# A Macaron block on one core: the last three tiles of every expert part put behind a branch

## The chip, the cores and the metric

One core of a Trainium2 chip runs the whole block. The metric is the device time in microseconds of one execution. The kernel before was run three times: 655.76, 656.89 and 658.45 us, median 656.89. A separate execution under the profiler gives the page and the trace.

## The reference

16 sequences of 256 tokens with 128 features, so 4096 tokens. Three steps, each added to the tokens:

```python
x = x + 0.5 * ffn(layernorm(x))
x = x + attention(layernorm(x))      # 16 heads of 8, causal
x = x + 0.5 * ffn(layernorm(x))

def ffn(flat):                       # 8 experts, 256 hidden, best 2 of 8 for each token
    probs = softmax(flat @ gate_w.T)
    weights, idx = top_k(probs, 2)
    weights = weights / sum(weights)
    combine = sum(one_hot(idx, 8) * weights[..., None], axis=1)
    h1, h3 = einsum('nd,ehd->neh', flat, w1), einsum('nd,ehd->neh', flat, w3)
    y = einsum('neh,edh->ned', silu(h1) * h3, w2)
    return einsum('ned,ne->nd', y, combine)
```

The reference runs all eight experts on every token. The kernel runs only the two that each token chose, so it sorts the tokens by expert on the chip. Everything is computed in 32-bit floats, apart from masks and counts.

## The kernel before, in words

The tokens stay in SBUF as eight blocks of 512. Each of the two feed-forward steps is cut into three parts, each with its own routing: blocks 0, 1 to 3 and 4 to 7 before the attention (`ahead`), blocks 0 to 3, 4 to 6 and 7 after it (`after`). A part has a scratch tensor in DRAM for the sorted inputs (`part.x`, in the trace `rows_x`) and one for the experts' outputs (`part.y`, `rows_y`).

*Routing* (`route_in_steps`, lines 330 to 441) finds each token's two experts, counts them per expert, and gives each of the two choices a row in `part.x`. An expert's rows start at a new tile of 128 rows, so its last tile is filled up with rows that no token owns. How many tiles this takes depends on the data; with `ht` tiles of tokens it can't exceed `2 * ht + 7`, and that is the number of tiles that the kernel always runs (`part.nj`, line 59): 15, 31 and 39 tiles for parts of 1, 3 and 4 blocks, 170 over both steps. `upto` holds the running sum of tiles over the experts. From it lines 421 to 434 make `eji`, the expert of each tile; tiles past the last counted one are given to expert 7, run on zeros or left-over rows, and nobody reads their outputs.

*Scatter* (line 449): POOL writes the normalised tokens to their rows, 128 rows for each indirect transfer, two transfers for each tile of tokens. *Experts* (lines 466 to 592): tiles go through in groups of three. SP loads a group (`xg`), PE transposes it (`px`), ACT copies it (`xgT`); for each tile DVE copies the chosen expert's first weights (`wt`, line 502; the expert's number comes from `eji` through a register load, line 483), PE multiplies (`ph`, line 514), ACT and DVE make `silu(h1) * h3` (`gt`, lines 525 and 536), PE multiplies with the second weights (`py`, line 544), ACT copies a group's result and sends it to `part.y` (lines 554 and 555). *Combine* (lines 595 to 623): POOL gathers each token tile's two output rows (`yt`, line 611), and DVE adds them, weighted, to the tokens (line 602), four gathers behind.

`experts_of` (line 655) interleaves a part's tiles with other work. Each turn emits one tile, then one step of `aside` (routing of another part, a piece of the attention's opening), then `rate(j)` transfers from `beside` (the scatter of a later part's rows, or the gathers of an earlier part). A transfer is preceded by a one-element memset called `tick`, which is emitted even when no transfer is left. At turn `part.nj` the next part is prepared by `then()`: its first loads, its first transposes, its first two weight copies. Before this, with `ahead`, all transfers are emitted. After the last turn the remaining transfers are emitted in any case (line 710). Inside these stages the order on PE, POOL, DVE and ACT is the order of emission; SP's order is left to the scheduler.

The last stages, lines 1252 to 1274: the tiles of `after[0]` run beside the scatters for the two later parts, the tiles of `after[1]` beside the gathers of `after[0]`, the tiles of `after[2]` beside the gathers of `after[1]`; then the gathers of `after[2]` follow. Finished blocks are stored by SP (line 1196).

Of the kernel before, what the change touches and what calls it, by code (L numbers as in the profile page):

```python
# [11 lines left out]
FP = mybir.dt.float32  # L12
BF = mybir.dt.bfloat16
I32 = mybir.dt.int32
AF = mybir.ActivationFunctionType
ALU = mybir.AluOpType
# [3 lines left out]
P = 128  # L20
NB, SEQ, D = 16, 256, 128
NH, DK = 16, 8
NE, NHID = 8, 256
NHC = NHID // P
# [11 lines left out]
HT = NT // 2  # L36
JG = 3
NJG = 13


class InTurn:


    def __init__(self, *pools):
        self.pools = itertools.cycle(pools)
# [5 lines left out]
class Part:  # L51


    def __init__(self, first, blocks, scratch):
        self.first, self.blocks = first, blocks
        self.ht = blocks * TPB


        self.nj = 2 * self.ht + NE - 1
        self.ng = -(-self.nj // JG)  # L60
        self.x, self.y = scratch


# [4 lines left out]
def macaron_kernel(  # L68
# [15 lines left out]
    nc = tc.nc  # L84
# [4 lines left out]
    work = ctx.enter_context(tc.tile_pool(name="work", bufs=2))  # L89
# [20 lines left out]
    def load_x(*blocks):  # L110
        for t in blocks:
            nc.sync.dma_start(
                out=xs[t], in_=x[ts(t, BLK), :].rearrange("(c p) d -> p c d", p=P)
            )


    def scratch(name, blocks):
        rows = Part(0, blocks, (None, None)).nj * P
        return tuple(tc.dram_tile([rows, D], FP, name=f"{name}_{s}") for s in "xy")

    places = [scratch(f"rows{i}", n) for i, n in enumerate((1, 3, 4))]
    ZW = 16
    zeros = const.tile([P, ZW * D], FP)
    nc.vector.memset(zeros, 0.0)

    def clear(i, queue=nc.sync):
        rows = places[i][0].rearrange("(p c) d -> p (c d)", p=P)
        n = rows.shape[1]
        for at in range(0, n, ZW * D):
            w = min(ZW * D, n - at)  # L130
            queue.dma_start(out=rows[:, at : at + w], in_=zeros[:, 0:w])
# [8 lines left out]
    w13_f = w13_sb.rearrange("d e w h -> d (e w h)")  # L140
    w2_f = w2_sb.rearrange("p c e d -> p (c e d)")
# [2 lines left out]
    nc.sync.dma_start(out=w2_sb, in_=w2)  # L144
    clear(1)
    load_x(4, 5, 6, 7)
    wq_in = const.tile([D, NG, 4, 32], FP)
    wk_in = const.tile([D, NG, 4, 32], FP)
    wv_sb = const.tile([D, D], FP)
# [7 lines left out]
    ident = const.tile([P, P], FP)  # L157
# [5 lines left out]
    for e in range(NE):  # L163
# [7 lines left out]
        out=before_f,  # L171
        in_=before_f,
# [13 lines left out]
    for blocks in (1, 3, 4):  # L186
        n = blocks * TPB
# [142 lines left out]
    def route_in_steps(part, ps, fine=False, placed_at=None):  # L330
# [33 lines left out]
        rest = new("rest")  # L364
# [7 lines left out]
        d = new("d", [P, ht])  # L372
# [19 lines left out]
        upto = new("upto", [P, NE])  # L392
# [15 lines left out]
        rows = new("rows", [P, 2, ht])  # L408
# [8 lines left out]
        if placed_at is not None:  # L417
            placed_at(rowi)
        yield

        grid = [1, part.ng * 4, NE]
        past = work.tile([1, NJG * 4, NE], FP, tag="g_past", name="past")[:, 0 : part.ng * 4, :]
        nc.vector.tensor_tensor(
            past,
            jgrid[:, 0 : part.ng * 4, :],
            upto[0:1, :].unsqueeze(1).to_broadcast(grid),
            ALU.is_ge,
        )
        if fine:
            yield  # L430
        ej = work.tile([1, NJG * 4], FP, tag="g_ej", name="ej")[:, 0 : part.ng * 4]
        nc.vector.tensor_reduce(ej, past, AX.X, ALU.add)
        eji = work.tile([1, NJG * 4], I32, tag="g_eji", name="eji", bufs=3)
        nc.vector.tensor_scalar(eji[:, 0 : part.ng * 4], ej, float(NE - 1), None, ALU.min)

        den = new("den", [P, ht])
        nc.vector.tensor_scalar(den, ex, 2.0, 2.0, ALU.mult, ALU.add)
        c = new("c", [P, 2, ht], bufs=3)
# [27 lines left out]
    def experts(part, eji):  # L466
# [6 lines left out]
        def load(g):  # L473
            xg = work.tile([P, JG, D], FP, tag="xg", name="xg", bufs=3)
            n = tiles(g)
            nc.sync.dma_start(
                out=xg[:, 0:n, :],
                in_=part.x[g * JG * P : (g * JG + n) * P, :].rearrange("(c p) d -> p c d", p=P),
            )
            loaded[g] = xg  # L480
# [57 lines left out]
        def project(j):  # L538
# [12 lines left out]
            if c == tiles(g) - 1:  # L551
# [7 lines left out]
                    in_=yg[:, 0:n, :],  # L559
                )  # L560

        def fetch():
            load(0)
            load(1)
# [8 lines left out]
        def run():  # L573
            for j in range(part.nj + 2):
                made.at = j
                ph = hidden(j) if j < part.nj else None
                if j < part.nj and j % JG == 0:
                    g = j // JG
                    if g + 2 < part.ng:
                        load(g + 2)  # L580
                    if g + 1 < part.ng:
                        turn(g + 1)
                if j + 2 < part.nj:
                    weigh(j + 2)
                if ph is not None:
                    gated(j, ph)
                if 0 <= j - 2:
                    project(j - 2)
                yield

        made = SimpleNamespace(part=part, fetch=fetch, begin=begin, tiles=run(), begun=False, by_tanh=False)
        return made


# [60 lines left out]
    def experts_of(  # L655
        work,
        beside,
        aside=iter(()),
        side=(0, 0),
        pulls=lambda j: 1,  # L660
        rate=lambda j: 1,
        then=None,
        opened=None,
        ahead=True,
    ):

        following = None

        def transfer():
            nc.gpsimd.memset(tick, 0.0)  # L674
            return next(beside, done)

        done = object()
        with opened or ExitStack() as stack:
            one = 1 if side[1] else 2
            if opened is None:  # L680
                banks = expert_banks(stack, one, 3 if side[1] else 4)
            else:
                banks = work.banks
                more = psum(stack, "ps_h2", 2)
                banks.h = InTurn(banks.h, more)
            if side[0]:
                pools["first"], pools["banks"] = psum(stack, "ps_f", 1), side[0]
            if side[1]:
                pools["side"] = psum(stack, "ps_m", side[1])
            stack.enter_context(manual())  # L690
            if not work.begun:
                work.fetch()
                work.begin(banks)
            work.banks = banks
            for _ in work.tiles:
                j = work.at
                for _ in range(pulls(j)):
                    next(aside, None)
                for _ in range(rate(j) if j >= 2 else 0):
                    transfer()  # L700
                if j == work.part.nj:
                    for _ in aside:
                        pass
                    while ahead and transfer() is not done:
                        pass
                    if then is not None:
                        following = then()
                        following.fetch()
                        following.begin(banks)
            while transfer() is not done:  # L710
                pass
        return following

# [322 lines left out]
    after = [Part(0, 4, places[2]), Part(4, 3, places[1]), Part(7, 1, places[0])]  # L1036
# [155 lines left out]
    def back(part, route, after_block):  # L1192
        return combine(part, route[0], route[2], after_block)

    def store(t):
# [4 lines left out]
    none = lambda t: None  # L1200
    opening, steps, left_routes, left_moves = attention(after)
    tiles = experts(ahead[0], routes[0][1])
    tiles = experts_of(
        tiles,
        second,
        others(),
        (0, 2),
        rate=lambda j: 2,
        then=lambda: experts(ahead[1], routes[1][1]),
    )  # L1210
    tiles = experts_of(
        tiles,
        scatter(ahead[2], xns, routes[2][0]),
        constants(),
        rate=lambda j: 2,
        then=lambda: experts(ahead[2], routes[2][1]),
    )
# [2 lines left out]
        itertools.chain(back(ahead[0], routes[0], none), back(ahead[1], routes[1], none)),  # L1220
        opening(),
        (2, 1),
        pulls=lambda j: int(j >= 14),
    )

    left, right = ExitStack(), ExitStack()
# [20 lines left out]
    with manual():  # L1247
# [4 lines left out]
    tiles = experts_of(  # L1252
        behind[0],
        following(left_moves),
        ending,
        (0, 2),
        rate=lambda j: 2,
        then=lambda: experts(after[1], left_routes[1][1]),
        opened=opened,
    )  # L1260
    tiles = experts_of(
        tiles,
        back(after[0], left_routes[0], store),
        then=lambda: experts(after[2], left_routes[2][1]),
        ahead=False,
    )
    experts_of(
        tiles,
        back(after[1], left_routes[1], store),
        rate=lambda j: 1 + (j % 3 == 0),  # L1270
        ahead=False,
    )
# [42 lines left out]
```

## Time and profile before

| | |
|---|---|
| median of three runs | 656.89 us |
| the profiled execution's own time | 657.1 us |
| its span, first to last instruction | 655.1 us |
| mean granted PE clock | 0.965 |
| PE busy / PE weight loads | 576.9 us (88%) / 484.4 us (74%) |
| DVE / ACT / POOL busy | 448.2 (68%) / 352.7 (54%) / 419.7 (64%) |
| scatter transfers, issue on POOL (L449) | 128, 988 ns each |
| gather transfers, issue on POOL (L611) | 128, 975 ns each |
| group loads `xg` / output writes `rows_y` | 58 each, of them 56 of 192 KB: 2.9 / 2.1 us to landing |

The expert parts lie at about 47 to 79, 79 to 125 and 125 to 202 us, then the attention until about 494 with the first tiles of the next part already among its last batch, then 478 to 560, 560 to 606 and 606 to 629 us, and a tail to 655. Busy shares over the whole span mix these stages, which don't have the same limit; they are best read stage by stage. PE, DVE, ACT, POOL and SP are the five engines; a name with a q is the engine's sequencer or DMA queue. In a timeline row the number in brackets is the idle time of the engine before the row, with what ended it by the profile.

### The profile page before, as it was taken

The page shows a single profiled execution, that of the slowest core. Times are in us where ns is not written, and L with a number is a line of the kernel's source. Part 1 is how long each engine was busy: PE and PEld are TensorE (multiplying, and loading weights), DVE is VectorE, ACT ScalarE, POOL GpSimd, SP SyncE. Part 2 cuts the span into 40 slices and gives each one's busy share as a digit, 9 for nine tenths or more (in the row PEclk, how much of TensorE's full clock was granted, in tenths as well). Part 3 has the DMA queues.
Part 4 walks back from the last instruction along what each step waited for, and adds up shares of the span by engine and source line. Part 5 has one row for each costly group of instructions (what it writes and reads, how often), then busy time and mean ns, then how long its engine had stood idle before and what let it go on. Part 6 is the DMA issues. An engine that isn't in the chain of part 4 may idle for free.

```text
span 655.1 us, 17006 instructions
## 1 busy us (share of the span) xinstructions
PE 576.9 (88%) x6158; PEld 484.4 (74%) x6158; DVE 448.2 (68%) x1405; ACT 352.7 (54%) x730; POOL 419.7 (64%) x862
## 2 busy tenths in 40 slices
PE   4369799999998999999999999999998799999930
PEld 3258699999986677777777766777677799999930
DVE  7754765566665788888887899677646556576742
ACT  6245444446623667777686866675646345444410
POOL 3568889767532666666663437788710884787785
PEclk9989999999996999999999999999999979999985
DMA  8726444454310000000000000000112333456442
GB/s 301 276 86 225 131 125 130 134 137 107 78 42 20 19 14 20 18 18 15 18 18 3 2 2 23 29 30 36 58 38 60 110 110 94 131 148 165 122 121 72
DMA packets 65905, 53.73 MB, mean 82 GB/s; under 512 B 6560, under 2 KB 60576, under 8 KB 65312
## 3 DMA queue, kind: packets, MB, share of 16 engines
q1 hardware_dynamic: 34368, 22.16, 10.8%
q0 software_dynamic: 8192, 16.79, 8.6%
q10 hardware_dynamic: 23264, 13.71, 7.1%
q8 instruction: 50, 0.82, 0.5%
q14 instruction: 31, 0.25, 0.1%
HBM read 25.43 MB, written 27.20 MB: 80 GB/s over the span
## 4 chain that ended last, share of the span: by engine, by line
PE 70%; POOL 8%; DVE 8%; issue 5%; ACT 5%; DMA 2%; DVEq 1%; ACTq 0%; POOLq 0%; SPq 0%
PE ph L514 18%; PE sm L782 12%; PE py L544 8%; PE o L887 7%; PE sw L797 6%; PE sm L809 6%; POOL rows_x L449 4%; PE pl L315 3%; POOL yt L611 3%; PE px L493 2%; PE pt L302 2%; DVE top L813 2%; ACT pT L823 1%; PE pm L868 1%; PE po L925 1%
## 5 line engine op out<-in xcount | busy, mean ns | idle before, releaser
L514 PE MATMUL ph<-xgT,wt 128*128 128x128 f32 x1360 | 184.9, 280 | 8.6 <-DVE wt L502 6.7
L514 PEld LDWEIGHTS ph<-xgT,wt 128*128 128x128 f32 x1360 | 169.3, 196 | 11.7 <-DVE wt L502 5.5
L825 POOL TENSOR_SCALAR_AFFINE_SELECT pT<-pT 128x256 f32<-128x256 f32 x256 | 100.0, 414 | 107.4 <-ACT pT L823 106.3
L813 DVE TENSOR_REDUCE top<-sm 128x3 f32<-128x384 f32 x256 | 130.3, 551 | 54.5 <-PE sm L809 51.4
L449 POOL DMA_INDIRECT rows_x<-xn,rowi x128 | 126.5, 988 | 47.7 <-issue 22.6
L823 ACT ACTIVATE pT<-sw 128x768 f32<-128x768 f32 x128 | 104.0, 812 | 86.2 <-PE sw L797 79.3
L611 POOL DMA_INDIRECT yt<-rows_y,rowi x128 | 124.9, 975 | 28.4 <-issue 15.9
L782 PE MATMUL sm<-kp,qp 32*128 32x256 f32 (+1 forms) x1024 | 127.9, 354 | 3.2 <-ACT kp L758 1.6
L525 ACT ACTIVATE gt<-ph 128x256 f32<-128x256 f32 x165 | 63.2, 384 | 117.4 <-PE ph L514 108.1
L797 PE MATMUL sw<-qm,kp 32*128 32x128 f32 (+1 forms) x1024 | 120.9, 354 | 1.1 <-ACT pT L823 1.1
L782 PEld LDWEIGHTS sm<-kp,qp 32*128 32x128 f32 x1024 | 95.1, 187 | 31.3 <-DVE top L813 10.6
L536 DVE TENSOR_TENSOR gt<-gt,ph 128x256 f32<-128x256 f32 x165 | 68.6, 416 | 59.9 <-ACT gt L525 59.2
L544 PE MATMUL py<-w_sb,gt 128*128 x680 | 104.6, 278 | 3.3 <-ACT yg L554 1.9
L502 DVE COPY wt<-w_sb 128x512 f32 x170 | 75.7, 448 | 36.1 <-issue 25.0
L544 PEld LDWEIGHTS py<-w_sb,gt 128*128 128x128 f32 x680 | 90.5, 194 | 4.1 <-ACT yg L554 2.3
L797 PEld LDWEIGHTS sw<-qm,kp 32*128 32x128 f32 x1024 | 68.6, 189 | 2.8 <-ACT pT L823 1.8
L602 DVE SCALAR_TENSOR_TENSOR x<-yt,c,x 128x128 f32<-128x128 f32 x128 | 45.7, 361 | 18.3 <-DMA yt<-rows_y,rowi 18.0
L887 PE MATMUL o<-pT,vaug 128*32 128x256 f32 (+1 forms) x1024 | 56.2, 335 | 0.0
L809 PE MATMUL sm<-mask_two,ident_b 128*128 128x256 bf16 x256 | 50.8, 281 | 0.0
L250 POOL TENSOR_TENSOR rstd<-ve,neg_half 128x4 f32<-128x4 f32 x24 | 25.3, 1054 | 39.6 <-DVE ve L248 38.7
L887 PEld LDWEIGHTS o<-pT,vaug 128*32 128x32 f32 x1024 | 27.7, 110 | 23.2 <-issue 9.6
L674 POOL MEMSET tick<- 128x1 f32 x269 | 37.3, 139 | 5.7
(124 smaller groups left out, 660.3 us busy)
## 6 DMA issues: line engine op xcount, KB each, us to landing
xg<-rows_x SPq DMA_DIRECT2D x56, 192.0 KB, 2.9
rows_y<-yg ACTq DMA_DIRECT2D x56, 192.0 KB, 2.1
w_sb<-in_w SPq DMA_DIRECT2D x3, 1024.0 KB
x<-in_x SPq DMA_DIRECT2D x8, 256.0 KB, 13.8
rows_x<-xn,rowi POOLq DMA_INDIRECT x128
rows_x<-zeros ACTq DMA_DIRECT2D x2, 1024.0 KB
yt<-rows_y,rowi POOLq DMA_INDIRECT x128
out_y<-x SPq DMA_DIRECT2D x8, 256.0 KB, 3.5
```

The lines of the kernel that those rows point to most:

```text
L449: i = nc.gpsimd.indirect_dma_start(out=part.x, out_offset=bass.IndirectOffsetOnAxis(ap=rowi[:, n, t : t + 1], axis=0), in_=xns[part.first ...
L502: nc.vector.tensor_copy(wt.rearrange("d k h -> d (k h)"), w13_f[:, bass.ds(es[g][c] * (2 * NHID), 2 * NHID)],)
L514: nc.tensor.matmul(out=ph[:, k // NHC, k % NHC, :], lhsT=wt[:, k, :], rhs=xTs[g][:, c, :], start=True, stop=True,)
L544: nc.tensor.matmul(out=ys[g][:, c, :], lhsT=gt[:, hc, :], rhs=w2_f[:, bass.ds(es[g][c] * D + hc * (NE * D), D)], start=(hc == 0), stop=(hc ...
L611: nc.gpsimd.indirect_dma_start(out=yt, out_offset=None, in_=part.y, in_offset=bass.IndirectOffsetOnAxis(ap=rowi[:, n, t : t + 1], axis=0),)
L782: nc.tensor.matmul(out=s[u][:, to], lhsT=qp[r, j, ts(q, P)], rhs=kp[r, SET[j], k], start=(q == 1), stop=False,)
L797: nc.tensor.matmul(out=s[:, u, to], lhsT=kp[r, SET[j], ts(k, P)], rhs=qm[r, j, q], start=True, stop=True,)
L809: nc.tensor.matmul(out=s[u][:, 128:384], lhsT=ident_b, rhs=mask_qk, start=False, stop=True)
L813: nc.vector.tensor_reduce(tops[b % 2][:, j, i0 + u, :], s[u][:, 0:384].rearrange("p (n k) -> p n k", k=P), AX.X, ALU.max,)
L823: nc.scalar.activation(pT, s[:, :, 0:384], AF.Exp, scale=DK**-0.5)
L825: nc.gpsimd.affine_select(out=pT[:, u, 0:256].rearrange("p (n q) -> p n q", q=P), in_=pT[:, u, 0:256].rearrange("p (n q) -> p n q", q=P), ...
L887: nc.tensor.matmul(out=o[32 * i : 32 * i + 32, j // 2, q], lhsT=va[:, kt, 4 * j + i, :], rhs=pTs[i // 2][:, i % 2, at], start=(j % 2 == 0 ...
```

## The change

A part now runs only `2 * ht + 4` tiles always (`part.nj`: 12, 28, 36). The three tiles that can come on top (`SPARE`) are a new function `rest`, whose body stands behind a branch: entered if the routing counted more than `part.nj` tiles. The count is one more element at the end of `eji`. The scratch tensors keep their size, and the last three tiles of each `part.y` are filled with zeros at the start. `experts_of` calls `rest` after a part's turns, before what transfers are left; all five engines load the count and branch. In the stage of `after[1]`'s tiles, the gathers of `after[0]` that are left over after the last turn are no longer emitted at its end (`all_of_them=False`) but come first beside the tiles of `after[2]`. The attention's opening is pulled from turn 11 instead of 14.

```diff
+SPARE = 3
...
-        self.nj = 2 * self.ht + NE - 1
+        self.most = 2 * self.ht + NE - 1
+
+        self.nj = self.most - SPARE
         self.ng = -(-self.nj // JG)
+        self.grid = -(-self.most // JG)
...
+    for _, y in places:
+        nc.sync.dma_start(
+            out=y[y.shape[0] - SPARE * P :, :].rearrange("(p c) d -> p (c d)", p=P),
+            in_=zeros[:, 0 : SPARE * D],
+        )
...
-        eji = work.tile([1, NJG * 4], I32, tag="g_eji", name="eji", bufs=3)
-        nc.vector.tensor_scalar(eji[:, 0 : part.ng * 4], ej, float(NE - 1), None, ALU.min)
+
+        eji = work.tile([1, NJG * 4 + 1], I32, tag="g_eji", name="eji", bufs=3)
+        nc.vector.tensor_scalar(eji[:, 0:n], ej, float(NE - 1), None, ALU.min)
+        nc.vector.tensor_copy(eji[:, NJG * 4 : NJG * 4 + 1], upto[0:1, NE - 1 : NE])
...
+        def rest():
+            counted = nc.values_load(
+                eji[0:1, NJG * 4 : NJG * 4 + 1],
+                min_val=0,
+                max_val=part.most,
...
+            )
+            banks = made.banks
+            few = range(part.nj, part.most)
+            rows = slice(part.nj * P, part.most * P)
+            with tc.If(counted > part.nj):
+                xg = work.tile([P, JG, D], FP, tag="xg", name="xg", bufs=3)
+                nc.sync.dma_start(
+                    out=xg, in_=part.x[rows, :].rearrange("(c p) d -> p c d", p=P)
+                )
+                px = banks.x.tile([P, JG, P], FP, tag="x", name="px")
+                for c in range(SPARE):
+                    nc.tensor.transpose(px[:, c, :], xg[:, c, :], ident)
+                xT = work.tile([D, JG, P], FP, tag="xgT", name="xgT", bufs=2)
+                nc.scalar.copy(xT, px)
+                wt = work.tile([D, SPARE, 2 * NHC, P], FP, tag="w_rest", name="w_rest", bufs=1)
+                py = banks.y.tile([P, JG, D], FP, tag="y", name="py")
+                for c, j in enumerate(few):
...
+                yg = work.tile([P, JG, D], FP, tag="yg", name="yg", bufs=3)
+                nc.scalar.copy(yg, py)
+                nc.scalar.dma_start(
+                    out=part.y[rows, :].rearrange("(c p) d -> p c d", p=P), in_=yg
                 )
...
+        all_of_them=True,
     ):
...
-            while transfer() is not done:
+            work.rest()
+            while all_of_them and transfer() is not done:
                 pass
...
-        pulls=lambda j: int(j >= 14),
+        pulls=lambda j: int(j >= 11),
...
+    gathers = back(after[0], left_routes[0], store)
     tiles = experts_of(
         tiles,
-        back(after[0], left_routes[0], store),
+        gathers,
         then=lambda: experts(after[2], left_routes[2][1]),
         ahead=False,
+        all_of_them=False,
     )
     experts_of(
         tiles,
-        back(after[1], left_routes[1], store),
+        itertools.chain(gathers, back(after[1], left_routes[1], store)),
         rate=lambda j: 1 + (j % 3 == 0),
         ahead=False,
     )
```

The tiles within the branch, left out above at the inner "...", do for each of the three what `turn`, `weigh`, `hidden`, `gated` and `project` do for a tile.

More of the change, by code (lines that the diff above doesn't have):

```diff
@@ L117, in scratch @@
     def scratch(name, blocks):
-        rows = Part(0, blocks, (None, None)).nj * P
+        rows = Part(0, blocks, (None, None)).most * P
         return tuple(tc.dram_tile([rows, D], FP, name=f"{name}_{s}") for s in "xy")
@@ L419, in route_in_steps @@
         yield
-        grid = [1, part.ng * 4, NE]
-        past = work.tile([1, NJG * 4, NE], FP, tag="g_past", name="past")[:, 0 : part.ng * 4, :]
+        n = part.grid * 4
+        grid = [1, n, NE]
+        past = work.tile([1, NJG * 4, NE], FP, tag="g_past", name="past")[:, 0:n, :]
         nc.vector.tensor_tensor(
             past,
-            jgrid[:, 0 : part.ng * 4, :],
+            jgrid[:, 0:n, :],
             upto[0:1, :].unsqueeze(1).to_broadcast(grid),
@@ L430, in route_in_steps @@
             yield
-        ej = work.tile([1, NJG * 4], FP, tag="g_ej", name="ej")[:, 0 : part.ng * 4]
+        ej = work.tile([1, NJG * 4], FP, tag="g_ej", name="ej")[:, 0:n]
         nc.vector.tensor_reduce(ej, past, AX.X, ALU.add)
-        eji = work.tile([1, NJG * 4], I32, tag="g_eji", name="eji", bufs=3)
-        nc.vector.tensor_scalar(eji[:, 0 : part.ng * 4], ej, float(NE - 1), None, ALU.min)
+        eji = work.tile([1, NJG * 4 + 1], I32, tag="g_eji", name="eji", bufs=3)
+        nc.vector.tensor_scalar(eji[:, 0:n], ej, float(NE - 1), None, ALU.min)
+        nc.vector.tensor_copy(eji[:, NJG * 4 : NJG * 4 + 1], upto[0:1, NE - 1 : NE])
         den = new("den", [P, ht])
@@ L560, in project @@
                 )
+        def rest():
[3 more added lines that the diff above has]
+                max_val=part.most,
+                skip_runtime_bounds_check_because="tiles are counted by the routing",
+            )
[15 more added lines that the diff above has]
+                for c, j in enumerate(few):
+                    at = 4 * (j // JG) + j % JG
+                    _, (e,) = nc.values_load_multi_w_load_instructions(
+                        eji[0:1, at : at + 1],
+                        engines=[mybir.EngineType.PE, mybir.EngineType.DVE],
+                        min_val=0,
+                        max_val=NE - 1,
+                        skip_runtime_bounds_check_because="the values are held within the experts",
+                    )
+                    nc.vector.tensor_copy(
+                        wt[:, c].rearrange("d k h -> d (k h)"),
+                        w13_f[:, bass.ds(e * (2 * NHID), 2 * NHID)],
+                    )
+                    ph = banks.h.tile([P, 2, NHC, P], FP, tag="h", name="ph")
+                    for k in range(2 * NHC):
+                        nc.tensor.matmul(
+                            out=ph[:, k // NHC, k % NHC, :],
+                            lhsT=wt[:, c, k, :],
+                            rhs=xT[:, c, :],
+                            start=True,
+                            stop=True,
+                        )
+                    gt = work.tile([P, NHC, P], FP, tag="gt", name="gt", bufs=4)
+                    nc.scalar.activation(gt, ph[:, 0], AF.Silu)
+                    nc.vector.tensor_tensor(gt, gt, ph[:, 1], ALU.mult)
+                    for hc in range(NHC):
+                        nc.tensor.matmul(
+                            out=py[:, c, :],
+                            lhsT=gt[:, hc, :],
+                            rhs=w2_f[:, bass.ds(e * D + hc * (NE * D), D)],
+                            start=(hc == 0),
+                            stop=(hc == NHC - 1),
+                        )
+                yg = work.tile([P, JG, D], FP, tag="yg", name="yg", bufs=3)
+                nc.scalar.copy(yg, py)
+                nc.scalar.dma_start(
+                    out=part.y[rows, :].rearrange("(c p) d -> p c d", p=P), in_=yg
+                )
@@ L589, in run @@
                 yield
-        made = SimpleNamespace(part=part, fetch=fetch, begin=begin, tiles=run(), begun=False, by_tanh=False)
+        made = SimpleNamespace(
+            part=part, fetch=fetch, begin=begin, tiles=run(), rest=rest, begun=False, by_tanh=False
+        )
         return made
```

## The prediction

> **What bounds the kernel now.** I read the chain of waits first, then the busy table by slices, cut again into this kernel's own stages, then the timelines of POOL and PE at the joints. I name the six expert parts A (15 tiles), B (31), C (39) before the attention and D (39), E (31), F (15) after it.
>
> ```profile
> PE 70%; POOL 8%; DVE 8%; issue 5%; ACT 5%; DMA 2%; DVEq 1%; ACTq 0%; POOLq 0%; SPq 0%
> ```
>
> PE carries 70% of the chain, so dropping 18 of 170 tiles looks large. A steady tile repeats every 1.45 us (in B, three tiles from 83.54 to 87.89: 4.35 us), so a part gives up 4.35 us where PE is last, six parts 26 us. The stages say where it is last (columns: stretch, length, busy us of PE, PE loads, DVE, ACT, POOL, granted clock, DMA share, GB/s; B, C, E, F, the end):
>
> ```profile
> 79.00:125.00 46.00, 45.28 (x402) 45.01 (x403) 26.64 (x90) 20.87 (x53) 40.03 (x107) 1.00 0.44 133
> 125.00:188.00 63.00, 61.87 (x529) 59.51 (x527) 42.95 (x130) 34.76 (x89) 40.97 (x87) 1.00 0.40 105
> 560.00:606.00 46.00, 44.92 (x404) 44.76 (x403) 31.40 (x88) 21.31 (x53) 37.08 (x75) 1.00 0.56 150
> 606.00:629.00 23.00, 22.08 (x192) 21.54 (x192) 16.16 (x48) 9.91 (x24) 17.90 (x34) 1.00 0.49 131
> 629.00:655.00 26.00, 0.00 (x0) 0.00 (x0) 6.68 (x19) 0.00 (x0) 16.67 (x26) 0.58 0.30 83
> ```
>
> In the last 26 us PE does nothing: POOL's gathers end the kernel. In B both PE and POOL are nearly full. POOL's timeline settles both places:
>
> ```profile
> 119.58 5.72 POOL L674 MEMSET tick<- 128x1 f32 x33
> ...
> 558.88 3.39 POOL L674 MEMSET tick<- 128x1 f32 x17
> 563.87 1.06 POOL L611 DMA_INDIRECT yt<-rows_y,rowi  x1 [1.59 <-DMA xg<-rows_x]
> ...
> 600.36 1.03 POOL L611 DMA_INDIRECT yt<-rows_y,rowi  x1 [2.09 <-DVE x L602]
> ...
> 609.42 1.04 POOL L611 DMA_INDIRECT yt<-rows_y,rowi  x1 [2.50 <-DVE wt L502]
> ...
> 648.57 0.95 POOL L611 DMA_INDIRECT yt<-rows_y,rowi  x1 [0.30 <-issue]
> ```
>
> B's companion, the scatter of C's rows, ends at 119.58; C's first rows are fetched at 121.45 and transposed at 124.30. From 563.87 there are 64 gathers, one each 1.255 us when nothing holds them: 63 steps, 79.1 us. They take 84.7 to the start of the last, so under 6 us of that stretch is waiting: 2.09 for a buffer that DVE frees late, 2.50 before gather 33, the first to need E's outputs.
>
> **Is the branch entered?** Routing the reference's inputs gives 12, 27, 35, 36, 27, 12 tiles with rows; the new caps are 12, 28, 36, 36, 28, 12. None exceeds its cap, so all six bodies are jumped over and 18 tiles are really gone.
>
> **What the tiles give, by part.** A: B's first rows wait for the scatter that POOL issues back to back from 49.99 to 72.97; it doesn't move. 0. B: C's rows wait for the scatter that starts at 76.06 and ends at 119.58. It follows A's ticks, six fewer x 0.154 = 0.9 us, against a crossing of about 1 us. 0; PE gets 4.35 us of slack. C: PE is busy 61.87 of 63, so 4.35 us come off; the attention opening is pulled three tiles earlier, so nothing of it is pushed past the end. D: it decides when the gathers start, and there POOL is last: the final scatter ends at 558.88 because its places come from the routing near tile 32 of D, which is kept. What goes is six of 17 ticks (3.39/17 = 0.20 each), 1.2 us, and the wait for D's outputs, which come 4.35 us earlier. E: its outputs come about 8 us earlier, so the two waits above go. F: outputs are ready some 15 us before gather 57 needs them. 0.
>
> **What a crossing adds.** Each engine loads the counted tiles into a register, compares, jumps to the other side, waits there for its own earlier work, jumps on. The load has a row, by the experts' numbers that PE and DVE load today (min/median/max ns):
>
> ```profile
> L483 DVEq TENSOR_LOAD <-eji x58: 623/804/2561, 20.8 to 618.9; - x58
> L483 PEldq TENSOR_LOAD <-eji x58: 308/790/2657, 21.0 to 617.6; - x58
> ```
>
> I take 0.8 us. The jumps have no row. [...]
>
> In the built order, the first matmul after the join waits on ACT, DVE and PE together, so I let PE wait for the last engine across. Where it is exposed:
> - C's start: ACT issues B's last output transfer at 125.63 + 0.34, then 1.0: 127.0, against PE's start at 125.42. **+1.6**.
> - C to attention: ACT's last transfer ends at 202.67, crossing 203.7; score matmuls at half clock follow (to about 205), and only then the table load of 1.28 us, which today runs beside them; the first exponential goes from 204.05 to about 206.3. **+2.2**.
> - A's: slack of B. PE will idle from about 72, where A's last tiles run today, until B's rows at 77.5. A gap of 4.27 us ahead of 524.70 shows what follows (columns as above):
>
> ```profile
> 522.00:524.00 2.00, 0.00 (x0) 0.00 (x0) 0.16 (x1) 0.60 (x2) 1.82 (x4) 0.95 0.08 33
> 524.00:526.00 2.00, 1.30 (x6) 1.30 (x7) 1.83 (x5) 1.28 (x4) 1.95 (x5) 0.50 0.15 53
> 526.00:528.00 2.00, 2.00 (x11) 2.00 (x11) 0.42 (x1) 0.89 (x3) 1.81 (x4) 0.50 0.52 154
> ```
>
> Half clock for some 7 us, 3.3 us lost. With the delayed start and a reload of ACT's table (1.28, moved from A) B loses about 4.5 of its 4.35 + 0.6: C still starts near 124.3.
> - POOL, the engine that ends the kernel, crosses three times on its path: full 1.0 at D (ticks wait for each other, so nothing covers the load), about 0.4 at E and at F, where a gather of 0.95 covers the rest.
>
> The three added writes of zeros (0.59 MB on SP's queue, ahead of the attention weights) take 1.5 us of a busy stretch at 380 GB/s; the weights are not used before 90 us, SP's next issue is at 31.84. 0. Moving leftover gathers doesn't shorten POOL's list: the built order has 32 gathers, E's crossing, 12, F's, 20. It merely lets F's weights and first tile pass ahead. 0. Six DVE copies of one element, near 0.2 us each: 0, under ACT's and PE's work.
>
> **Sum, against the profiled execution** (span 655.1, with 2.0 around it 657.1; median of the runs 656.9). C: -4.35 + 1.6 + 2.2 = -0.55. End: 558.88 + 2.2 ticks + 1.0 + 0.76 (the idle that a gather with many waits shows at 126.06) = 562.9; 32 gathers x 1.255 to 603.1; + 0.4 + 0.8 for gather 33, 604.3 (E's outputs land near 603); 39.15 more as today, + 0.4: the last starts at 643.9, not 648.57: -4.7. Together -5.2: **652**. Its own range is 648.5 to 655.5 (C and the end each off by 2).
>
> **Rivals.** [...] (2) *B ends early and PE's clock drops ahead of C.* If B keeps its slack, PE idles 4 us before 124.3 and C starts at half clock: +3.3, 655.3. For it: the rows above; against: the loss at A eats that slack. (3) *Crossings hide.* If PE needn't wait for ACT, C saves 4.35 - 0.4 - 1.0, and POOL's loads run under gathers and ticks: the end -5.8; 648.3. (4) *A body is entered*: where a part stands at its cap, no expert lies less than 5 rows from one more tile; then near +10.
>
> **Chances.** Forecast 0.48, (1) 0.24, (2) 0.13, (3) 0.13, (4) 0.02. This kernel can tell about 0.5% (3.3 us) from no change. Some 0.34 of the forecast's own lies below 653.6, with (3) 0.47 faster; 0.14 of it and most of (2), 0.26 the same; (1), (4) and a rest, 0.27 slower. The range 646.5 to 662 leaves out the upper part of (1) and little else.
>
> **What would show it.** Right: C's first tile still near 124; the first gather near 563, gather 33 near 604, no idle of 2 us within the gathers; PE idle and half clock about 77; POOL's hole at D 1 to 2 us. Wrong: holes of 3 us or more at crossings, C starting late, half clock at its start.

## The result, and the profile after

| | before | after |
|---|---|---|
| median of 20 runs | 657.35 us (653.50 to 662.53) | 655.23 us (650.23 to 663.13) |
| ratio | | 0.9955, 95% interval 0.9933 to 0.9977 |
| profiled execution / span | 657.1 / 655.1 us | 654.5 / 652.8 us |
| mean granted PE clock | 0.965 | 0.942 |
| PE busy | 576.9 us | 561.8 us |

By the ratio the change is worth about -3.0 us, -4.4 to -1.5 (the medians differ by 2.1). Medians are of all executions; ratios leave out the few that ran in a slower state. A second measurement of the same pair gave 0.9941 (0.9910 to 0.9973), -3.9 us. The forecast was -5.2 us and 652.0: the right side, inside the range, and at the edge of what can be told from no change. PE is busy 15 us less, and the kernel gains a fifth of it.

No body was entered: there are 1216 first-weight matmuls, 8 for each of 152 tiles. The stages again, of the kernel after (columns as before: stretch, length, busy us of PE, PE loads, DVE, ACT, POOL, granted clock, DMA share, GB/s; B, C, E, F, the end):

```profile
79.00:121.00 42.00, 41.76 (x357) 41.57 (x357) 22.62 (x82) 19.48 (x47) 36.40 (x97) 0.96 0.41 126
123.50:184.00 60.50, 59.27 (x489) 56.81 (x490) 38.74 (x119) 32.28 (x82) 37.59 (x69) 0.97 0.37 100
556.00:599.00 43.00, 42.53 (x364) 42.08 (x364) 27.22 (x77) 18.67 (x46) 34.61 (x71) 0.96 0.52 143
603.00:620.00 17.00, 16.86 (x140) 16.51 (x140) 12.05 (x34) 7.01 (x18) 14.27 (x26) 0.95 0.42 110
622.00:652.80 30.80, 0.00 (x0) 0.00 (x0) 8.22 (x24) 0.00 (x0) 20.82 (x34) 0.55 0.31 87
```

Each stage is shorter and none of these stretches has the full clock any more (0.95 to 0.97; before, 1.00 in all four); the joints between them are left out. PE's last matmul ends at 620.5 instead of 628.4 us, the span only 2.3 us sooner: POOL's gathers still close the kernel. POOL's timeline of the kernel after, at the places shown of before:

```profile
117.22 3.88 POOL L751 MEMSET tick<- 128x1 f32 x25
...
559.31 1.37 POOL L751 MEMSET tick<- 128x1 f32 x9
...
562.28 0.98 POOL L687 DMA_INDIRECT yt<-rows_y,rowi  x1 [0.91 <-DMA xg<-rows_x]
...
600.20 0.94 POOL L687 DMA_INDIRECT yt<-rows_y,rowi  x1 [3.18 <-DVEq L585]
...
607.21 0.94 POOL L687 DMA_INDIRECT yt<-rows_y,rowi  x1 [0.86 <-DVE x L678]
...
646.49 0.94 POOL L687 DMA_INDIRECT yt<-rows_y,rowi  x1 [0.30 <-issue]
```

The first gather is at 562.28; before it was at 563.87, and the forecast was 562.9. The wait ahead of gather 33 has shrunk from 2.50 to 0.86. The one ahead of gather 28 (600.20) was to go; it has grown from 2.09 to 3.18.

The crossings themselves, in the kernel after (count, then min/median/max in ns, first and last start):

```profile
L576 POOLq TENSOR_LOAD <-eji x6: 293/296/497, 72.4 to 620.6; - x6
L576 DVEq TENSOR_LOAD <-eji x6: 313/314/514, 74.1 to 620.7; - x6
L576 PEldq TENSOR_LOAD <-eji x6: 305/308/309, 75.7 to 619.9; - x6
L576 ACTq TENSOR_LOAD <-eji x6: 278/283/533, 78.2 to 621.5; - x6
```

```profile
L585 POOLq COMPARE_BRANCH  x6: 45/45/45, 73.0 to 621.0; - x6
L585 DVEq COMPARE_BRANCH  x6: 56/56/72, 74.4 to 621.1; - x6
L585 PEldq COMPARE_BRANCH  x6: 215/234/344, 76.1 to 620.3; - x6
L585 ACTq COMPARE_BRANCH  x6: 45/45/45, 78.8 to 621.9; - x6
```

By the medians a load of one value takes 0.28 to 0.31 us, and not the 0.8 of the row for three values; a compare and branch 0.05 to 0.06 us, on PE 0.23. No long hold at one shows: the longest of them lasts 0.34 us, and of the two queues that the page calls instruction, q8 moves 50 packets in both kernels, q14 33 against 31. So nothing is seen of (1), the slower kernel to which the prediction gave 0.24. An engine's own crossing is cheap: load and branch together are 0.33 to 0.37 us on POOL, ACT and DVE, 0.54 on PE. What follows is about what waits for it.

### The profile page after: what moved, and what is told of

Same layout as the page of the kernel before. It is cut to its first block, busy times and chain, and to the rows that moved or that the text cites. A ratio compares the mean times of both kernels' runs of the same rounds, so it can differ in the third digit from the quotient of the medians.

```text
span 652.8 us, 16461 instructions
## 1 busy us (share of the span) xinstructions
PE 561.8 (86%) x5924; PEld 466.2 (71%) x5924; DVE 434.4 (67%) x1375; ACT 340.4 (52%) x700; POOL 413.8 (63%) x840
## 5 line engine op out<-in xcount | busy, mean ns | idle before, releaser
L526 PE MATMUL ph<-xgT,wt 128*128 128x128 f32 x1216 | 171.6, 287 | 12.7 <-ACTq L585 6.6
L526 PEld LDWEIGHTS ph<-xgT,wt 128*128 128x128 f32 x1216 | 157.7, 202 | 16.1 <-ACTq L585 7.4
L537 ACT ACTIVATE gt<-ph 128x256 f32<-128x256 f32 x147 | 56.4, 383 | 112.1 <-PE ph L526 104.0
L548 DVE TENSOR_TENSOR gt<-gt,ph 128x256 f32<-128x256 f32 x147 | 61.2, 416 | 63.8 <-ACT gt L537 63.2
L556 PE MATMUL py<-w_sb,gt 128*128 x608 | 94.0, 279 | 2.1 <-ACT yg L566 1.9
L514 DVE COPY wt<-w_sb 128x512 f32 x152 | 66.8, 442 | 35.0 <-issue 23.8
L556 PEld LDWEIGHTS py<-w_sb,gt 128*128 128x128 f32 x608 | 81.4, 196 | 2.7 <-ACT yg L566 2.3
L505 PE MATMUL px<-ident,xg 128*128 128x128 f32 x152 | 28.6, 301 | 12.7 <-SPq L585 6.6
```

The costliest lines, as they stand in the source:

```text
L514: nc.vector.tensor_copy(wt.rearrange("d k h -> d (k h)"), w13_f[:, bass.ds(es[g][c] * (2 * NHID), 2 * NHID)],)
L526: nc.tensor.matmul(out=ph[:, k // NHC, k % NHC, :], lhsT=wt[:, k, :], rhs=xTs[g][:, c, :], start=True, stop=True,)
L548: nc.vector.tensor_tensor(gt, gt, ph[:, 1], ALU.mult)
L556: nc.tensor.matmul(out=ys[g][:, c, :], lhsT=gt[:, hc, :], rhs=w2_f[:, bass.ds(es[g][c] * D + hc * (NE * D), D)], start=(hc == 0), stop=(hc ...
```

## The experiments

Theory at the start: the crossings take the gain, through PE's wait for the other engines at each join. Rival: the clock takes it, crossing or not. Each ratio is to the kernel before, measured beside it.

**The crossings left out, and the crossings alone.** The first kernel doesn't call `rest`, so a part's optional tiles can't run at all. The second keeps all 170 tiles and places the same body, never entered, behind the same branch; it also keeps the change's small parts, the writes of zeros and the later place of leftover gathers, which the first kernel has too.

```diff
-            work.rest()
```

```diff
-        self.nj = self.most - SPARE
+        self.nj = self.most
...
-            few = range(part.nj, part.most)
-            rows = slice(part.nj * P, part.most * P)
+            few = range(part.nj - SPARE, part.nj)
+            rows = slice((part.nj - SPARE) * P, part.nj * P)
...
-        pulls=lambda j: int(j >= 11),
+        pulls=lambda j: int(j >= 14),
```

> The changed kernel without its six crossings: the 18 tiles and the branch are both gone, so a part that has more tiles than its cap would lose them (no part of these inputs has). Theory (crossings take the gain): the matmuls at each join no longer wait for ACT (1.3 us at C's start, 0.5 at the attention) and POOL no longer loads and jumps three times (0.5 each), so 2 to 4 us less than the changed kernel: ratio to before 0.989 to 0.992, about 650.5. Rival (clock): what the tiles gave is lost because PE idles at the joints and comes back at half clock, crossing or no crossing: within 1 us of the changed kernel, 0.994 to 0.997. [...]

> The kernel before with the six crossings alone: all 170 tiles are kept, and the body that is jumped over is still there. Theory (crossings take the gain): +1.3 to 1.6 us at C's start, +0.5 to 2.2 at the attention, +0.5 to 1.0 for POOL ahead of D's gathers, +0.4 at E: +3 to +5, ratio 1.004 to 1.008. Rival (clock): the crossings are hidden, 0.999 to 1.002. [...]

Measured: without crossings 646.72 us, ratio 0.983 (0.9777 to 0.9883), -11.2 us. Crossings alone 665.02 us, 1.0096 (1.0062 to 1.0129), +6.3 us. Both sides point the same way: the 18 tiles are worth 11 us, six crossings take back 6 to 8. The theory holds, with a price above the 2 to 4 us (first kernel) and 3 to 5 us (second) that it expected. The rival that put it all on the clock, crossing or not, is out by both kernels. That the clock has a share in the price is shown below.

In these traces the cost shows in two places. PE at C's start, first the kernel after, then without crossings:

```profile
121.25 0.55 PE L505 MATMUL px<-ident,xg 128*128 128x128 f32 x3 [0.49 <-SPq L585]
...
123.55 2.07 PE L526 MATMUL ph<-xgT,wt 128*128 128x128 f32 x8 [1.31 <-ACTq L585]
```

```profile
121.64 0.55 PE L505 MATMUL px<-ident,xg 128*128 128x128 f32 x3 [0.53 <-DMA xg<-rows_x]
...
122.76 1.16 PE L526 MATMUL ph<-xgT,wt 128*128 128x128 f32 x8
```

From the transposes to the first tile it takes 2.30 us with the crossing, 1.12 without: PE waits for ACT to come across. And then eight matmuls take 2.07 us and not 1.16, about half speed. The windows of PE there, the kernel after and then without crossings:

```profile
122.00:126.00 4.00, 2.69 (x14) 2.50 (x13) 0.47 (x2) 0.83 (x3) 3.04 (x6) 0.69 0.76 196
126.00:130.00 4.00, 4.00 (x34) 4.00 (x33) 2.30 (x6) 1.53 (x5) 3.59 (x8) 0.88 0.40 103
```

```profile
122.00:126.00 4.00, 3.88 (x33) 3.55 (x32) 1.83 (x6) 1.96 (x5) 3.26 (x6) 1.00 0.78 194
126.00:130.00 4.00, 4.00 (x38) 4.00 (x37) 2.50 (x8) 1.89 (x5) 3.53 (x7) 1.00 0.53 142
```

In these 8 us 48 matmuls are done instead of 71, at a granted clock of 0.69 and 0.88. C's last output copy, at 195.18 without crossings, starts 2.26 us later with them.

The two halves of this cost are not equally firm. The wait is in all five traces of these measurements with a crossing at C's start: 2.30 to 3.12 us from transposes to first tile, by the last engine across, which is ACT in two and DVE in three; without one it is 1.12 in four traces and 1.65 in the fifth. The low clock followed in three of the five. In the kernel without POOL's crossing, measured later, PE waits longer and then starts at full speed (granted clock 1.00):

```profile
123.87 1.13 PE L526 MATMUL ph<-xgT,wt 128*128 128x128 f32 x8 [2.02 <-DVEq L591]
```

So the gap alone doesn't settle the clock, and the 2.26 us are those of one pair of traces: C's last output copy starts 3.4 us after 195.18 in the changed kernel's second trace (198.57) and 0.8 in the trace of this row (195.95).

The second place is ACT between C's last output and the attention's first exponential, the kernel after, then without crossings:

```profile
197.44 0.48 ACT L566 COPY yg<-py 128x384 f32<-128x384 f32 x1 [8.48 <-PE py L556]
197.95 0.37 ACTq L567 DMA_DIRECT2D rows_y<-yg  x1
201.01 1.28 ACT L901 ACT_TABLE_LOAD   x1 [3.08 <-PE sw L875]
202.30 0.81 ACT L901 ACTIVATE pT<-sw 128x768 f32<-128x768 f32 x1
```

```profile
195.18 0.48 ACT L566 COPY yg<-py 128x384 f32<-128x384 f32 x1 [8.47 <-PE py L556]
195.69 0.37 ACTq L567 DMA_DIRECT2D rows_y<-yg  x1
196.14 1.28 ACT L900 ACT_TABLE_LOAD   x1 [0.48 <-ACT yg L566]
197.44 0.81 ACT L900 ACTIVATE pT<-sw 128x768 f32<-128x768 f32 x1
```

From copy to exponential: 4.86 us with the crossing, 2.26 without (and 2.26 in the kernel before). The table load, 1.28 us, ran beside the score matmuls `sw`; now it comes after them. That is +2.60, by the mechanism that the prediction worked out (+2.2). In the six traces of these measurements with a crossing behind C it takes 4.85 to 4.90 us, in the four without 2.26. Of the 6.65 us between the last gathers of these two traces, 4.86 are there at the first exponential and 5.29 at the first gather; the last 1.36 arise within the gathers.

**Half of the change at a time.** A part gets its three tiles' branch or keeps its old count, before the attention alone or after it alone.

```diff
-    def __init__(self, first, blocks, scratch):
+    def __init__(self, first, blocks, scratch, spare=SPARE):
...
-        self.nj = self.most - SPARE
+        self.spare = spare
+        self.nj = self.most - spare
...
-            work.rest()
+            if work.part.spare:
+                work.rest()
```

with `spare` 0 for `after` in the first kernel, for `ahead` in the second (there the attention's opening is pulled from turn 14 again).

> Fewer tiles and a crossing in A, B and C alone; D, E and F are as before. By the prediction's sum -0.55 us (C -4.35, its start +1.6, the attention +2.2): ratio 0.998 to 1.000. By the changed kernel's trace, whose attention starts 2.7 us earlier: -2.7 us if that stays (0.996), 0 if it is lost on the way to D's last scatter (1.000).

> Fewer tiles and a crossing in D, E and F alone; A, B and C are as before. By the prediction's sum -4.7 us: ratio 0.993. By the changed kernel's trace, where gather 28 waits 3.2 us and the gathers start 1.6 earlier: -2 to -2.5 us, 0.996 to 0.997.

Measured: A, B and C alone 657.87 us, 0.9991 (0.9973 to 1.0008), -0.6 us; the prediction's sum gives -0.55. D, E and F alone 654.25 us, 0.9923 (0.9899 to 0.9947), -5.1 us by the ratio and -3.5 by the medians; the prediction's sum gives -4.7. The figures taken from the changed kernel's trace (-2 to -2.5) are outside the interval. That the sum's -4.7 fits is in part luck: in this kernel's trace gather 28 still waits 3.18 us, and from first to last gather it takes 84.4 us, not the 81.0 of the sum. The halves add to -5.7, the whole gave -3.0 and -3.9: with about 2 us of uncertainty on the sum that may be chance, and it stays open.

How far one trace can mislead is seen in a stretch whose work is the same in these kernels, the end of the attention with D's first tiles. From POOL's first scatter for D to its first for E it takes 110.6 us in the kernel before and 113.5 in the kernel after; 109.6 with D, E, F alone, 113.7 with A, B, C alone, and 113.2 in the kernel without crossings. The windows, the kernel after and then D, E and F alone:

```profile
461.78:477.78 16.00, 13.87 (x139) 8.61 (x136) 8.84 (x28) 8.63 (x15) 8.50 (x18) 0.81 0.21 64
477.78:493.78 16.00, 16.00 (x140) 13.03 (x138) 7.46 (x22) 6.88 (x13) 3.27 (x8) 0.87 0.09 26
```

```profile
464.55:480.55 16.00, 13.83 (x158) 9.25 (x156) 9.30 (x29) 9.71 (x18) 8.76 (x18) 1.00 0.21 64
480.55:496.55 16.00, 16.00 (x168) 13.08 (x165) 8.99 (x27) 8.99 (x17) 3.26 (x8) 1.00 0.13 38
```

PE is equally busy, 13.87 and 16.00 us of 16, yet does 279 matmuls in one and 326 in the other: the granted clock is 0.81 and 0.87 against 1.00. In a second profiled execution of the kernel after it took 111.1, in three later kernels 109.6 to 111.2. So up to 4 us of this stretch come and go with the clock. What sets the clock from one execution to the next no run here shows. The profile's own -2.3 us holds this +2.8: it says less about the change than the many runs do.

**What POOL's crossing costs, what holds gather 28, and a smaller set of branches.** Four kernels: the counted tiles loaded on four engines only, so that POOL has no load and no compare; the same with `spare` 0 for A, B and F; ten buffers for gathered rows; and A's eight gathers issued twice, into a tile that nobody reads.

```diff
                 eji[0:1, NJG * 4 : NJG * 4 + 1],
+                engines=[
+                    mybir.EngineType.PE,
+                    mybir.EngineType.DVE,
+                    mybir.EngineType.Activation,
+                    mybir.EngineType.SP,
+                ],
```

```diff
-                yt = work.tile([P, D], FP, tag="yt", name="yt", bufs=8)
+                yt = work.tile([P, D], FP, tag="yt", name="yt", bufs=10)
```

```diff
+                if part.ht == TPB and after_block is none:
+                    again = work.tile([P, D], FP, tag="again", name="again", bufs=2)
+                    nc.gpsimd.indirect_dma_start(
+                        out=again,
...
                 late.append((t, n, yt))
```

> The changed kernel, with the counted tiles loaded on PE, DVE, ACT and SP alone: the body has nothing for POOL, so POOL no longer loads, compares and jumps. Theory (POOL's share of a crossing is small in the tail: in the trace without crossings the gathers start 0.3 us earlier after the last scatter and run 1.4 us shorter): 0.5 to 1.7 us below the changed kernel, ratio 0.993 to 0.995. Rival (POOL's three crossings cost what the prediction charged, 1.8 us, and more where they stall): 0.990 to 0.992. Rival (PE's wait for ACT is all of it): no change, 0.9955.

> A candidate: three tiles fewer and a crossing in C, D and E alone; A, B and F keep all their tiles and have no crossing; POOL crosses nowhere. By the prediction's terms: C -4.35 + 2.2 (the attention) without the 1.6 at C's start, the end as in the run with D, E and F alone or a little better: -7 to -8 us, ratio 0.988 to 0.990, below every kernel that has the branch so far. Rival (clock): C still starts at half clock or the attention gives it back: 0.992 to 0.993, as D, E and F alone.

> The changed kernel with ten buffers for the gathered rows, not eight. It asks what holds gather 28 of the last stage for 3.2 us (in the kernel before 2.1). Theory (buffer): it waits for a buffer that DVE frees late; with two more the wait goes from gather 28 and is under 1 us there or two gathers later, and the time falls by 1 to 3 us. Rival (not the buffer: in the order as built gather 28 needs DVE's add 20, which ended 4.4 us before it starts): the same gather waits the same 3 us, the time is as the changed kernel's, 0.9955.

> The changed kernel with each of A's eight gathers (in C's stretch) issued a second time into a tile that nobody reads: eight more indirect transfers of POOL ahead of the last stage. Theory (the wait at gather 28 belongs to the count of POOL's transfers, as it is the 220th in all six kernels so far, with and without crossings, with E ending at different places): it moves to gather 20 of the last stage. Rival (it belongs to the place: DVE's adds and copies at the end of E's tiles): it stays at gather 28. Time: about the changed kernel's, up to 3 us more.

In this measurement everything was slower: the kernel before took 769.57 us, and the mean clock of the four was 0.88 to 0.91. The ratios, 0.9837 (0.9784 to 0.9889), 0.9958 (0.9932 to 0.9984), 0.9867 (0.9803 to 0.9930), and 766.57 us for one execution of the last, can't be set against the earlier ones. Among themselves they say that nine tiles fewer (0.9958) gain less there than eighteen (0.9837); for POOL's share they say nothing.

The lower clock is only a part of it. The kernel without POOL's crossing was measured again later, with the same instructions: its traces span 757.5 and 649.3 us, 108 apart, with PE busy 602.3 and 558.1, 44 apart. The rest is idle time. PE stands still for 43 us in the slow trace, and 0.9 in the other, while it waits for nothing that the profile shows. The largest group (us in total, times, longest):

```profile
PE ph L526 <- issue: 14.9, 15, 4.4
```

What held PE there stays open. This measurement and the one before it carry the same chip number, 6, so another chip isn't shown to be the cause.

The question of gather 28 they do answer. In the kernel before, the profile names DVE's add as the releaser. DVE frees the buffer that gather 28 takes with its 20th add. DVE's timeline of the kernel before has the 20th add of the stage here:

```profile
597.22 0.35 DVE L602 SCALAR_TENSOR_TENSOR x<-yt,c,x 128x128 f32<-128x128 f32 x1
```

It ended at 597.57; gather 28 started at 600.36, 2.8 us later. So it was not held by that buffer. With ten buffers the same gather again waits 3.18 us. Nor is it a crossing: without crossings it waits nearly as long.

```profile
594.67 0.94 POOL L687 DMA_INDIRECT yt<-rows_y,rowi  x1 [3.01 <-DVE wt L514]
```

And it is always POOL's 220th indirect transfer: with eight more ahead of the stage, in the one execution of that kernel, the wait goes to gather 20, which is then the 220th. POOL's timeline there (687.49 is gather 18):

```profile
687.49 0.94 POOL L687 DMA_INDIRECT yt<-rows_y,rowi  x1 [1.07 <-DVE x L678]
688.43 0.28 POOL L759 MEMSET tick<- 128x1 f32 x1
688.74 0.94 POOL L687 DMA_INDIRECT yt<-rows_y,rowi  x1
689.68 0.11 POOL L759 MEMSET tick<- 128x1 f32 x1
692.05 0.94 POOL L687 DMA_INDIRECT yt<-rows_y,rowi  x1 [2.25 <-DVE wt L514]
693.00 0.11 POOL L759 MEMSET tick<- 128x1 f32 x1
693.30 0.94 POOL L687 DMA_INDIRECT yt<-rows_y,rowi  x1 [0.19 <-issue]
```

The add that gather 20 needs ended at 689.58, so this too is no wait for a buffer; and gather 28 of that kernel waits under 0.8 us. The 220th transfer is held by 1.7 to 3.2 us in all 14 traces of this case. It is not the count of POOL's instructions of every kind that matters: 795 of the engine's instructions start ahead of the 220th transfer in the kernel before and 775 in the kernel after. What in POOL's or its queue's state it is remains open; the releasers that the profile names (an add, a weight copy, a crossing) are merely what ended just before.

**POOL's crossing and the smaller sets, measured together.** The kernel after, the one without POOL's crossing, the one with branches in C, D and E, and one with branches in D and E only:

> The changed kernel itself, as the measure for the three beside it: the four runs before these met a chip on which the kernel before took 769.6 us, so that their ratios cannot be set against the changed kernel's 0.9955. Both theories: 0.9955 on a chip as the first; about 0.985 on one as the second, where PE's clock is lower and 18 tiles fewer weigh more.

> The changed kernel without POOL's load, compare and jump. Theory (POOL's share of a crossing is small): 0.5 to 1.7 us below the changed kernel beside it, ratio lower by 0.001 to 0.0025. Rival (POOL's three crossings cost 1.8 us and more where they stall): lower by 0.004 or more. Rival (PE's wait for ACT is all of it): the same.

> Three tiles fewer and a crossing in C, D and E alone, none on POOL. By the terms that the runs showed (C -4.35, the attention's crossing +2.6 and no crossing at C's start, where it cost 2.3; the end as with D, E and F alone): -7 us, ratio 0.988 to 0.990, and below the changed kernel by 0.005 to 0.007. Rival (A's and B's three tiles carry part of the gain): between the changed kernel and D, E and F alone, 0.992 to 0.9955.

> Three tiles fewer and a crossing in D and E alone, none on POOL; the part before the attention is the kernel before's. Theory (each part's tiles and its own crossing add up): as D, E and F alone or up to 1.5 us better, 0.990 to 0.992; C's -1.75 (its tiles less the attention's crossing) is what the run with C, D and E must have over it. Rival (F's tiles matter to the end): above 0.994.

| branches in | POOL crosses | median us | ratio (95%) |
|---|---|---|---|
| all six | yes | 655.17 | 0.9941 (0.9910 to 0.9973) |
| all six | no | 653.68 | 0.9921 (0.9891 to 0.9950) |
| C, D, E | no | 654.11 | 0.9925 (0.9892 to 0.9959) |
| D, E | no | 653.63 | 0.9938 (0.9904 to 0.9972) |

For all four the interval lies below 1, and they can't be told from each other. POOL's crossing costs what the theory gave it (0.002, expected 0.001 to 0.0025), but the intervals allow both rivals too, nothing and 0.004; in the traces the last scatter's start to the first gather is 3.8 us without and 4.0 with it. For D and E alone 0.9938 lies between the theory's 0.990 to 0.992 and the rival's (above 0.994), and its interval holds both. The candidate with C, D and E missed the 0.988 to 0.990 that its terms gave: its 0.9925 is in the rival's range, though the interval begins at 0.989. One trace shows where that execution lost it: in it the first exponential comes at 204.08, where the kernel before has it at 204.05. The 2.60 of the crossing are there again (199.22 to 204.08); and B lost what C saved. B's first 12 us, with branches in C, D and E, then in D and E:

```profile
78.00:90.00 12.00, 12.00 (x87) 12.00 (x87) 6.37 (x35) 4.44 (x11) 10.63 (x29) 0.79 0.40 125
```

```profile
78.00:90.00 12.00, 12.00 (x110) 12.00 (x108) 8.88 (x46) 5.68 (x14) 10.59 (x29) 1.00 0.47 145
```

The same work, without a crossing ahead of it in either: 87 matmuls and 110, clock 0.79 and 1.00. PE's gaps ahead of it (from 71 to 78 us) are the same in both to 0.01 us: 0.42, 1.37, 0.24 and 0.57. So the clock differs here without any difference in the program, and C's first tile comes 2.5 us later (126.14 and 123.61). Whether the other executions behind the median lost it in the same way isn't shown. No kernel with the branch was shown to beat the changed one; only leaving the branch out was, and that kernel is no longer right for every input.

## Why the prediction was right, and where it was wrong

- **The branch is not entered; 18 tiles go.** Right.
- **The tiles' worth.** The terms ahead of any crossing sum to -4.35 at C and -6.5 at the end (-4.7 less the 1.8 put in for POOL), -10.9; without crossings -11.2 was measured. The agreement is in part luck. The hold at gather 28 stayed (3.01 us), and first to last gather took 82.9 us, not the sum's 80.2. In return C's first tile came at 122.76, 2.7 us ahead of before's 125.42, where the sum had 0 for B.
- **The crossings' worth.** The terms sum to 1.6 + 2.2 + 1.8 = 5.6; measured +6.3 alone, and 8 as the difference to the kernel without.
- **The price of one** was 1.0 us. No run shows this term for an engine's own crossing, and +1.6, +2.2 and POOL's 1.8 contain it: load and branch together, by their medians, are 0.33 to 0.37 us on POOL, ACT and DVE, 0.54 on PE. The row from which the load was taken at 0.8 loads three values, and the jumps had no row. POOL's hole at D was to be 1 to 2 us; it is 0.45 us between the ticks and 0.91 ahead of the gather. The first gather at 562.28 is near the forecast by luck: with C's -0.55 the sum puts it at 562.35, and POOL's smaller hole made up for a last scatter of D that came 0.4 us later than before, after the attention's end had run at the lower clock shown above.
- **C's start, +1.6.** Against the kernel without crossings 2.3 at C's last output, in one pair of traces. The wait is there, 1.2 us from transposes to first tile in this trace and up to 2.0 in others; the rest is the low clock (0.69 and 0.88 over those 8 us) that rival 2 put ahead of C, with a chance of 0.13. The prediction thought it unlikely because PE wouldn't idle 4 us; here it came with gaps of 0.49 and 1.31 us, and in two other traces it stayed away with 1.8 and 2.0.
- **B, 0.** The sum put C's first tile at 127.0 (125.42 + 1.6); it came at 123.55. The scatter of C's rows ended 2.4 us earlier than before (117.2, was 119.6). In the kernels with D, E, F and with D, E alone, which have the same tiles in A and B as before, it ended at 118.0 and 117.9: most of this is no gain of the change but a late scatter in the one trace of before.
- **The attention, +2.2.** 2.6, by the mechanism named: the table load comes after the score matmuls.
- **A to B.** Right: PE idles 6.13 us ahead of B's rows (75.45), the first tile is at 79.00 at half clock (0.50 over 78 to 82 us), and before it was at 79.09.
- **The end, -4.7: the step that failed.** Of both waits within the gathers the prediction said that they go. Gather 33 was forecast for 604.3 and is at 607.21. The wait ahead of gather 28 is 3.18 us, longer by 1.1 instead of gone, since it was never a wait for E or for a buffer. From first to last gather the sum had 81.0 us, the trace 84.2: 3.2 us too few, and this term alone is larger than the 2.2 us by which forecast and measurement differ.
- **Rival 3** (crossings hide, 648.3) is out by the kernel with crossings alone (+6.3 us); of (1) and of rival 4 nothing appeared.

## What to carry to other kernels

A branch around a body that isn't entered costs little on the engine that crosses it, 0.33 to 0.54 us here, but it is a join: what ran beside other engines' work (here a table load, +2.60 us; a copy, 0.4 us; an early tile, +1.18 us) is put behind it, and a wait of PE may bring a lower clock behind it (0.50 to 0.75 in three of five traces). Price the join at each place by what waits for the last engine across; in the pair of traces read here two of six places held most of the price. Before a wait is booked as going away, find the instruction that it waits for and check that it ended late: a releaser that the profile names is only what came last. And where the granted clock differs between executions of the same instructions, 3 us between two traces are no evidence; take medians of many runs for the size and the traces for the place.

## What was not expected of the hardware

- The granted clock isn't settled by the gaps. After PE's wait at C's crossing it was 0.50 to 0.75 in the next 2 us in three traces (waits of 1.30 to 2.16 us) and 1.00 in two (1.82 and 2.02). Two kernels with the same instructions up to there and the same gaps to 0.01 us had 0.50 and 1.00 over 78 to 82 us. At the attention's end the same work took 109.6 to 113.7 us.
- In the trace of the kernel after, a compare-and-branch takes 45 ns on POOL and ACT, 45 to 50 on SP, 56 to 72 on DVE and 215 to 344 on PE. The longest of the 30 is one of PE's.
- POOL's 220th indirect transfer is held 1.7 to 3.2 us in every trace of this case. In the one kernel with eight more transfers ahead of it the hold follows the count, not the place.
- The kernel before took 657 to 658 us in three measurements and 770 in another, at mean clocks of 0.953 to 0.975 and of 0.896 to 0.921. Besides the clock, PE stood still there for nothing that the profile shows (43 us against 0.9 in two traces of one kernel). The cause is open.
